# Triangle attention and window scan on one core: scores, biases and row maxima in one VectorE operation, and the output projection moved to the mixed values' bank

## The chip, the cores and the metric

The kernel runs on one core of a Trainium2 chip. The metric is the device time of one execution in microseconds (us). A core has five engines, each with its own queue of instructions that it works off in order: TensorE (PE; its weight loads are listed apart as PEld), VectorE (DVE), ScalarE (ACT), GpSimd (POOL) and SyncE (SP), which here issues most of the DMA transfers. An instruction that needs another engine's result waits for a semaphore, and all that stands behind it in its queue waits too.

## The reference

The input `x` is an image of 256 x 256 positions with 128 channels. Two layers are applied, each as `x = x + layer(group_norm(x))`. Layer 0 is a triangle attention: each of the 256 rows of the image attends within itself, with 4 heads of 32 channels, and one bias per head and pair of positions is shared by all rows.

```python
# layer 0, xn: (1, 256, 256, 128) after a layer norm
tri_bias  = jnp.einsum('bijd,dh->bhij', xn, w_tri)[:, None]
mask_bias = INF * (mask[:, :, None, None, :] - 1.0)
q = (xn @ w_q).reshape(B, I, J, H, C) * (1.0 / np.sqrt(C))
k = (xn @ w_k).reshape(B, I, J, H, C)
v = (xn @ w_v).reshape(B, I, J, H, C)
scores = jnp.einsum('bimhc,binhc->bihmn', q, k) + tri_bias + mask_bias
attn = jax.nn.softmax(scores, axis=-1)
o = jnp.einsum('bihmn,binhc->bimhc', attn, v)
g = jax.nn.sigmoid((xn @ w_g + b_g).reshape(B, I, J, H, C))
o = (g * o).reshape(B, I, J, H * C)
return o @ w_o + b_o
```

Layer 1 cuts the image into windows of 8 x 8, runs a convolution and a selective scan with 16 states over each window in four orders, and gates and projects the result. All data is float32. The change concerns layer 0 alone.

## The kernel before, in words

The kernel has these stages, one after the other: statistics of the input (`bn_stats` over all of `x`), the layer norm of layer 0 with the triangle bias (the normalised image goes to DRAM as `xn_d`), the attention, and layer 1 with its scan. On the page the attention lies between about 540 and 2,735 us, layer 1 from about 2,800 us to the end.

In the attention a `Row` is one row of the image (256 positions) and a `Pair` is two rows (512 positions), since the projections to queries, keys, values and gates work on 512 columns at once. What a pair does: `load` brings `xn` and the mask, `queries`, `keys`, `values` and `gates` are matmuls on TensorE, and the functions of the same names with `_out` take their results out of PSUM. What a row does:

- `bias` (GpSimd, L449) adds the triangle bias and the mask bias of the row into `tm`, 8 blocks of 128 x 256: 4 heads, and two halves of the row's queries.
- `scores` (TensorE, L462) computes queries times keys into two PSUM tiles `sc0` and `sc1`, two heads each (4 blocks of 256 columns).
- `add(hp)` (VectorE, L472) adds `tm` to the scores of one tile, 128 x 1024 elements, into `at` in SBUF.
- `peak(hp)` (VectorE, L480) takes the negated maximum of each of the 4 blocks into `nmax`.
- `exps` (ScalarE, L488) computes the exponential of each block with `nmax` as bias, and the block's sum through ScalarE's accumulator.
- `turn(hp)` (TensorE, L516) transposes the blocks, two heads at a time, into the tiles `aT_p0` and `aT_p1`; `turn_out` copies one of them with VectorE (L528) and the other with ScalarE (L530).
- `mix` (TensorE, L539) multiplies by the values into the pair's `o_p`.
- `invert` (VectorE, L498) and `widen` (GpSimd, L503) make the reciprocal sums and spread them over the head's channels; `shares` (TensorE, L409) turns them for a pair, and `shares_out` (VectorE, L416) multiplies them into the gate.
- For a pair, `gather` (VectorE, L420) multiplies the mixed values by the gate, `project` (TensorE, L424) is the output projection into `y_p`, `project_out` (VectorE, L427) adds bias and residual, and `store` takes statistics and writes the rows to DRAM. `logistic` (ScalarE, L131 to L133) is the sigmoid of the gate.

The order of all this is written out by hand, under `tc.manual_schedule()`: the instructions stand in the queues as the loop over `s` (one step for each row) issues them. In step `s` the row `s` (`now`) is added and exponentiated, row `s + 1` (`nxt`) gets its scores, row `s - 2` (`mid`) is turned, row `s - 3` (`old`) is mixed. The pairs' work is split over the even and the odd step: `ahead` is the next pair, `behind` the last one, `done` the one before that. Two steps are one pair.

All eight PSUM banks are taken: `sc0` and `sc1` two each, `aT_p0` and `aT_p1` one each, one for `o_p` (pool `ps_o`), and one side bank that the results of all projections pass through in turn:

```python
        def side0(name):
            return ps_m.tile([P, 512], F32, name=name, tag="m")
```

Each tenant of the side bank is written by TensorE and emptied by one copy or operation before the next one may be written. Before the change its tenants in a pair are `g_p`, `q_p` and `y_p` in the even step, and `k_p`, `rd_p` and `v_p` in the odd one.

Of the kernel before, what the change touches and what calls it, by code (L numbers as in the profile page):

```python
# [12 lines left out]
F32 = mybir.dt.float32  # L13
AF = mybir.ActivationFunctionType
ALU = mybir.AluOpType
AX = mybir.AxisListType
# [3 lines left out]
P = 128  # L20
# [4 lines left out]
HC = 32  # L25
# [42 lines left out]
def kernel(  # L68
# [28 lines left out]
    nc = tc.nc  # L97
# [31 lines left out]
    def logistic(e):  # L129

        nc.scalar.activation(e, e, AF.Exp, scale=-1.0)  # L131
        nc.scalar.activation(e, e, AF.Ln, bias=one)
        nc.scalar.activation(e, e, AF.Exp, scale=-1.0)  # L133
# [34 lines left out]
    for dh in range(2):  # L168
        nc.scalar.dma_start(
            out=wtap[:, dh], in_=conv_w[:, dh * P : (dh + 1) * P].rearrange("t d -> d t")  # L170
# [5 lines left out]
    for dh in range(2):  # L176
        for k in range(KD):
            o, back = k % 2, k // 2
            for at, lo, n in (
# [5 lines left out]
                    out=wx[:, dh, o, at : at + n],  # L185
# [4 lines left out]
    for back in range(2):  # L190
        at = 32 * back
        nc.scalar.dma_start(
            out=wdt[at : at + DTR], in_=dt_w[:, 2 * back : 2 * back + 2]
        )
        for o in range(2):
            for dh in range(2):
                j = 2 * (o + 2 * back) + dh
                nc.scalar.dma_start(
                    out=wdt[at + DTR : at + DTR + 1, o, dh * P : (dh + 1) * P],
# [61 lines left out]
    with tc.tile_pool(name="lnc", bufs=1) as cp, tc.tile_pool(  # L261
        name="lnx", bufs=3
    ) as xp, tc.tile_pool(name="lnt", bufs=3) as tp, tc.tile_pool(
        name="lnp", bufs=2, space=PSUM
# [9 lines left out]
        for k in range(KD):  # L274
            for nh in range(2):
                for blk in range(NBLK):
                    nc.scalar.dma_start(
                        out=bdiag[k][nh][blk].rearrange("p t n -> p (t n)"), in_=zero
# [33 lines left out]
    with tc.tile_pool(name="atc", bufs=1) as cp, tc.tile_pool(  # L312
        name="atx", bufs=7
    ) as xp, tc.tile_pool(name="att", bufs=3) as tp, tc.tile_pool(
        name="ats", bufs=8
    ) as wp, tc.tile_pool(name="atps", bufs=1, space=PSUM) as ps_s, tc.tile_pool(
        name="atpt", bufs=1, space=PSUM
    ) as ps_t, tc.tile_pool(name="atpm", bufs=1, space=PSUM) as ps_m, tc.tile_pool(
        name="atpo", bufs=1, space=PSUM
# [11 lines left out]
        for mc in range(2):  # L331
            nc.sync.dma_start(
                out=trib[:, :, mc, :],
# [3 lines left out]
        def side0(name):  # L337
            return ps_m.tile([P, 512], F32, name=name, tag="m")

        class Pair:  # L340
# [24 lines left out]

            def queries_out(self):
                self.qs = tp.tile([P, 512], F32, name="qs")
                nc.scalar.mul(self.qs, self.q_p, 1.0 / math.sqrt(HC))

            def keys(self):  # L370
                self.k_p = side0("k_p")
# [48 lines left out]
                nc.vector.tensor_mul(self.og, self.o_p, self.gate)  # L420

            def project(self):
                self.y_p = side0("y_p")
                nc.tensor.matmul(self.y_p, wo, self.og, start=True, stop=True)  # L424

            def project_out(self):
# [8 lines left out]
        class Row:  # L435
# [32 lines left out]
                        )  # L468

            def add(self, hp):  # L470
                self.at[hp] = wp.tile([P, 4, IMG], F32, name="at")
                nc.vector.tensor_add(  # L472
                    self.at[hp],
                    self.sc[hp].rearrange("p h m n -> p (h m) n"),
                    self.tm[:, 4 * hp : 4 * hp + 4],
                )

            def peak(self, hp):
                self.nmax[hp] = wp.tile([P, 4], F32, name="nmax")
                nc.vector.tensor_reduce(  # L480
                    self.nmax[hp], self.at[hp], AX.X, ALU.max, negate=True
                )

            def exps(self, hp, js):
                if hp == 0 and js[0] == 0:
                    self.den = wp.tile([P, NH, 2], F32, name="den")
                for j in js:
                    nc.scalar.activation(  # L488
                        self.at[hp][:, j, :],
                        self.at[hp][:, j, :],  # L490
                        AF.Exp,
                        bias=self.nmax[hp][:, j : j + 1],
                        accum_out=self.den[:, 2 * hp + j // 2, j % 2 : j % 2 + 1],
                    )

# [36 lines left out]
            def mix(self):  # L532
                pair = self.pair
                if self.r == 0:
                    pair.o_p = ps_o.tile([P, 512], F32, name="o_p")
                for n in range(2):
                    for h in range(NH):
                        base = h * HC
                        nc.tensor.matmul(  # L539
                            pair.o_p[base : base + HC, self.row],  # L540
                            pair.vs[:, self.r, n, base : base + HC],
                            self.aT[h][:, n, :],
                            start=(n == 0),
                            stop=(n == 1),
                        )
# [4 lines left out]
        def pick(items, i):  # L550
            return items[i] if 0 <= i < len(items) else None

        with tc.manual_schedule():
            for pair in pairs[0:4]:
                pair.load()
            first = pairs[0]
            first.mask_bias()
            rows[0].bias()
            rows[1].bias()
            first.queries()  # L560
            first.queries_out()
            first.keys()
            first.keys_out()
            rows[0].scores()
            first.values()
            first.values_out()
            for s in range(n_rows + 4):
                sg, odd = divmod(s, 2)
                now, nxt, mid, old = (
                    pick(rows, s),  # L570
                    pick(rows, s + 1),
                    pick(rows, s - 2),
                    pick(rows, s - 3),
                )
                ahead, behind, done = (
                    pick(pairs, sg + 1),
                    pick(pairs, sg - 1),
                    pick(pairs, sg - 2),
                )
                if not odd:  # L580
                    if sg + 4 < n_pairs:
                        pairs[sg + 4].load()
                    if behind:
                        behind.load_residual()
                    if ahead:
                        ahead.mask_bias()
                if s + 2 < n_rows:
                    rows[s + 2].bias()
                if old:
                    old.mix()  # L590
                if now:
                    now.add(0)
                    now.peak(0)
                if mid:
                    mid.turn(0)
                if now:
                    now.exps(0, [0])
                if done:
                    if odd:
                        done.project_out()  # L600
                    else:
                        done.gather()
                if mid:
                    mid.turn_out(0)
                if now:
                    now.exps(0, [1, 2, 3])
                if odd and ahead:
                    ahead.keys()
                    ahead.keys_out()
                if not odd and behind:  # L610
                    behind.gates()
                    behind.gates_out()
                if now:
                    now.add(1)
                if mid:
                    mid.turn(1)
                    mid.turn_out(1)
                if now:
                    now.peak(1)
                if odd and behind:  # L620
                    behind.shares()
                    behind.shares_out()
                if not odd and ahead:
                    ahead.queries()
                    ahead.queries_out()
                if now:
                    now.exps(1, [0, 1, 2, 3])
                if nxt:
                    nxt.scores()
                if odd and ahead:  # L630
                    ahead.values()
                    ahead.values_out()
                if not odd and done:
                    done.project()
                if odd and done:
                    done.store()
                if not odd and behind:
                    logistic(behind.gate)
                if 0 <= s - 1 < n_rows:
                    rows[s - 1].invert()  # L640
                    rows[s - 1].widen()
# [636 lines left out]
    with tc.manual_schedule():  # L1278
# [37 lines left out]
        for i, unit in enumerate(units):  # L1316
            j, place = divmod(i, per_job)
# [102 lines left out]
```

## Time and profile before

| | us |
|---|---|
| Time before, median of 3 runs (24,755.36 to 24,756.92) | 24,756.14 |
| Profiled execution: time | 24,756.32 |
| Profiled execution: span from first to last instruction | 24,754.5 |
| Busy over the whole span: PE / DVE / ACT / POOL | 23,738.4 / 22,137.9 / 18,874.1 / 21,878.7 |
| L488 (exponentials, ACT), 2,048 instructions | 1,019.2 |
| L480 (maxima, DVE), 512 instructions | 622.0 |
| L472 (additions, DVE), 512 instructions | 614.4 |
| L449 (biases, POOL), 256 instructions | 1,166.3 |

A line of the page's groups reads: source line, engine, operation, names of the output and the inputs, their shapes, the number of instructions; then busy us in total and mean ns of one; then the engine's idle time just before them, and what ended most of it. A line of the waits reads: who waited, for whom, us in total, times, longest. A line of the timeline reads: start in us from the span's beginning, duration in us, engine, line, operation, names, shapes, and in brackets the idle time before it and what ended it. The record of one instruction reaches a little beyond the start of the next one on the same engine, so a sum of records is larger than the time that they take; starts to next starts are the better price. PEclk is the granted TensorE clock as a share of full speed.

### The profile page before, as it was taken

What the parts mean: (1) busy time and instruction counts of PE and PEld (TensorE: products, weight loads), DVE (VectorE), ACT (ScalarE), POOL (GpSimd) and SP (SyncE); (2) the same over time, 40 slices, a digit from 0 to 9 for tenths busy, and PEclk for the clock granted to TensorE, in tenths of its full rate; (3) what the DMA queues carried; (4) which work ended last, traced back from release to release, by engine and by line L of the source; (5) the groups of instructions that cost most, each with busy time, mean ns of one, the idle gap of its engine ahead of it and who ended that gap; (6) DMA issues with size and microseconds to landing.
All of it is one profiled execution on the core that took longest, in us unless ns stands there. A gap on an engine that the chain in (4) does not pass through costs nothing.

```text
span 24754.5 us, 429436 instructions
## 1 busy us (share of the span) xinstructions
PE 23738.4 (96%) x171020; PEld 17003.5 (69%) x171020; DVE 22137.9 (89%) x14740; ACT 18874.1 (76%) x35334; POOL 21878.7 (88%) x10062
## 2 busy tenths in 40 slices
PE   7888899999999999999999999999999999999999
PEld 2555577777777777777777777777777777777776
DVE  6888899999999999999999999999999999999998
ACT  5777777777777777777777777777777777777776
POOL 3666699999999999999999999999999999999999
PEclk9999999999999999999999999999999999999999
DMA  5222344444444444444444444444444444444444
GB/s 192 63 63 62 101 155 156 156 153 155 155 155 154 152 155 156 156 155 152 155 155 155 155 154 154 156 156 154 153 154 156 155 154 155 153 155 156 155 154 143
DMA packets 2000343, 3638.88 MB, mean 147 GB/s; under 512 B 1129584, under 2 KB 1131760, under 8 KB 1725824
## 3 DMA queue, kind: packets, MB, share of 16 engines
q1 hardware_dynamic: 1985616, 3602.35, 43.1%
q8 instruction: 1346, 22.05, 0.4%
q10 hardware_dynamic: 12720, 9.07, 0.1%
q14 instruction: 661, 5.41, 0.1%
HBM read 3467.33 MB, written 143.65 MB: 146 GB/s over the span
## 4 chain that ended last, share of the span: by engine, by line
PE 82%; DVE 8%; ACT 6%; issue 2%; POOL 1%; DMA 0%; ACTq 0%; SPq 0%; DVEq 0%; POOLq 0%
PE b_p L1173 31%; PE y_p L1206 28%; DVE h L1189 5%; PE cv_p L762 5%; PE dt_p L1011 4%; ACT at L488 2%; PE xd_p L942 2%; PE dut_p L1045 2%; PE in_p L717 1%; PE o_p L878 1%; PE y_p L1064 1%; PE z_p L796 1%; PE u_p L915 1%; PE sc L462 1%; POOL h L1195 1%
## 5 line engine op out<-in xcount | busy, mean ns | idle before, releaser
L1195 POOL TENSOR_TENSOR h<-h,cc 128x1024 f32<-128x1024 f32 x8192 | 19182.8, 2369 | 1524.1 <-DVE h L1189 1514.1
L1189 DVE TENSOR_TENSOR_SCAN h<-da,b_p 128x1024 f32<-128x1024 f32 x8192 | 18346.7, 2274 | 2068.7 <-PE b_p L1173 2011.5
L1160 ACT ACTIVATE da<-dt,am 128x508 f32<-128x508 f32 x16384 | 10663.9, 708 | 1910.4 <-DVE h L1189 1899.3
L1173 PE MATMUL b_p<-diag,dut 64*128 64x256 f32 x65536 | 9139.4, 401 | 388.2 <-DVE h L1189 386.8
L1206 PE MATMUL y_p<-ident,h 128*128 128x128 f32 x65536 | 8168.1, 278 | 7.7 <-POOL h L1195 7.6
L1206 PEld LDWEIGHTS y_p<-ident,h 128*128 128x128 f32 x65536 | 7207.2, 142 | 1406.7 <-issue 1062.0
L1173 PEld LDWEIGHTS b_p<-diag,dut 64*128 64x128 f32 x65536 | 5700.1, 186 | 3303.5 <-issue 1848.3
L734 ACT ACTIVATE tap<-xin,wtap 128x512 f32<-128x512 f32 x2048 | 1519.6, 742 | 0.5
L762 PE MATMUL cv_p<-ident,tap 128*128 128x128 f32 x9216 | 1446.1, 280 | 31.1 <-ACT tap L734 27.1
L1021 ACT ACTIVATE sp<-dt_p 128x512 f32<-128x512 f32 x1024 | 610.3, 596 | 1079.2 <-PE dt_p L1011 1078.4
L1034 POOL TENSOR_TENSOR du<-dt,u 128x512 f32<-128x512 f32 x1024 | 1308.6, 1278 | 59.9 <-DMA z<-bt 57.0
L762 PEld LDWEIGHTS cv_p<-ident,tap 128*128 128x128 f32 x9216 | 1037.9, 141 | 390.4 <-issue 204.9
L1151 ACT ACTIVATE da<-ident 128x16 f32<-128x16 f32 x1536 | 349.3, 227 | 1202.2 <-DVE h L1189 1202.1
L488 ACT ACTIVATE at<-at,nmax 128x256 f32<-128x256 f32 x2048 | 1019.2, 501 | 240.0 <-DVE nmax L480 240.0
L449 POOL TENSOR_TENSOR tm<-trib,mb 128x2048 f32<-128x2048 f32 x256 | 1166.3, 4556 | 10.7
L1011 PE MATMUL dt_p<-xd,wdt 9*128 9x512 f32 x2048 | 1149.6, 641 | 2.5 <-DVE dt L1027 2.2
L503 POOL COPY wide<-rden 128x256 f32<-128x256 f32 x256 | 101.6, 397 | 828.5 <-DVE rden L498 826.6
L1054 ACT COPY dut<-dut_p 128x512 f32<-128x512 f32 x1024 | 589.0, 575 | 256.9 <-PE dut_p L1045 245.2
L1022 ACT ACTIVATE sp<-sp,one 128x512 f32<-128x512 f32 x1024 | 739.6, 722 | 33.7
L1027 DVE SCALAR_TENSOR_TENSOR dt<-sp,dt_p 128x512 f32<-128x512 f32 x1024 | 677.9, 662 | 15.4 <-DMA z<-bt 11.5
L516 PEld LDWEIGHTS aT_p<-ident,at 128*128 128x128 f32 x4096 | 450.8, 141 | 343.0 <-issue 142.6
L472 DVE TENSOR_TENSOR at<-sc,tm 128x1024 f32<-128x1024 f32 x512 | 614.4, 1200 | 57.7 <-POOL wide L503 30.3
(132 smaller groups left out, 16405.1 us busy)
## 6 DMA issues: line engine op xcount, KB each, us to landing
cc<-c_d SPq DMA_DIRECT2D x2048, 1024.0 KB
diag<-z SPq DMA_DIRECT2D x1024, 1024.0 KB
xt<-in_x_dram SPq DMA_DIRECT2D x16, 2048.0 KB
xt<-in_x_dram SPq DMA_DIRECT2D x32, 1024.0 KB
xn_d<-xn SPq DMA_DIRECT2D x32, 1024.0 KB
xn<-xn_d SPq DMA_DIRECT2D x128, 256.0 KB
mb<-in_mask_dram SPq DMA_DIRECT2D x128, 256.0 KB
xr<-in_x_dram SPq DMA_DIRECT2D x128, 256.0 KB
```

The lines of the kernel that those rows point to most:

```text
L449: nc.gpsimd.tensor_add(self.tm, trib.rearrange("p h m n -> p (h m) n"), self.pair.mb[:, self.row].unsqueeze(1).to_broadcast([P, 2 * NH, IMG]),
L488: nc.scalar.activation(self.at[hp][:, j, :], self.at[hp][:, j, :], AF.Exp, bias=self.nmax[hp][:, j : j + 1], accum_out=self.den[:, 2 * hp ...
L734: nc.scalar.activation(scaled.rearrange("p s (y x) -> p s y x", x=WIN), self.xin[:, dh] .rearrange("p y f x -> p (y f) x")[:, 2 * dy : 2 * ...
L762: nc.tensor.matmul(cv_p[:, s], now[:, s], ident, start=(tap == 0 and s == 0), stop=(tap == 8 and s == GS - 1), is_transpose=True, skip_gro ...
L1011: nc.tensor.matmul(token_order(self.dt_p), wdt[rows, self.o, dh * P : (dh + 1) * P], token_blocks(self.xd[rows]), start=True, stop=True,)
L1022: nc.scalar.activation(sp, sp, AF.Ln, bias=one)
L1034: nc.gpsimd.tensor_mul(token_blocks(du), token_order(self.dt[back][dh]), token_blocks(self.u[:, dh]),)
L1160: nc.scalar.activation(da[:, :, j, lo:hi], dt[:, :, lo:hi], AF.Exp, scale=am[:, a0 : a0 + 1])
L1173: nc.tensor.matmul(b_p[:, s, :, h * 64 : (h + 1) * 64].rearrange("p n t -> p t n"), job.dut[self.back][rows, p, h, self.dh * P : (self.dh ...
L1189: nc.vector.tensor_tensor_scan(out=out_, data0=d0, data1=d1, initial=0.0, op0=ALU.mult, op1=ALU.add)
L1195: nc.gpsimd.tensor_mul(self.h, self.h, cc.rearrange("p n s t -> p s n t"))
L1206: nc.tensor.matmul(job.y_p[:, 2 * p + s, self.dh * P : (self.dh + 1) * P], self.h[:, s, j], ident, start=(first and s == 0 and j == 0), st ...
```

## The change

`add` no longer issues one addition over four blocks followed by `peak`'s maximum. It issues four `tensor_tensor_reduce`, one for each block of 128 x 256: the block is the sum of scores and biases, times -1, and the smallest of these negated sums, which is the negated maximum, goes to `nmax`. `exps` gets `scale=-1.0` so that the exponential is taken of the same number. `peak` is gone. The scaled copy of the queries `qs` goes from ScalarE to VectorE.

The order is changed as well: `y_p` is written to the bank of `o_p` (both have the tag "o", one buffer), `project` and `project_out` follow `queries_out` in the even step, `keys` goes from the odd step to the end of the even one, and `shares` goes ahead of `turn(1)` in the odd step, while `shares_out` stays behind `turn_out(1)`. The side bank's tenants are now `g_p`, `q_p`, `k_p` in the even step and `rd_p`, `v_p` in the odd one. Nothing else differs; layer 1 and the stages ahead of the attention are untouched.

```diff
--- before.py
+++ after.py
@@ -365,7 +365,9 @@
 
             def queries_out(self):
                 self.qs = tp.tile([P, 512], F32, name="qs")
-                nc.scalar.mul(self.qs, self.q_p, 1.0 / math.sqrt(HC))
+                nc.vector.tensor_scalar(
+                    self.qs, self.q_p, 1.0 / math.sqrt(HC), None, ALU.mult
+                )
 
             def keys(self):
                 self.k_p = side0("k_p")
@@ -420,7 +422,8 @@
                 nc.vector.tensor_mul(self.og, self.o_p, self.gate)
 
             def project(self):
-                self.y_p = side0("y_p")
+
+                self.y_p = ps_o.tile([P, 512], F32, name="y_p", tag="o")
                 nc.tensor.matmul(self.y_p, wo, self.og, start=True, stop=True)
 
             def project_out(self):
@@ -468,18 +471,20 @@
                         )
 
             def add(self, hp):
+
                 self.at[hp] = wp.tile([P, 4, IMG], F32, name="at")
-                nc.vector.tensor_add(
-                    self.at[hp],
-                    self.sc[hp].rearrange("p h m n -> p (h m) n"),
-                    self.tm[:, 4 * hp : 4 * hp + 4],
-                )
-
-            def peak(self, hp):
                 self.nmax[hp] = wp.tile([P, 4], F32, name="nmax")
-                nc.vector.tensor_reduce(
-                    self.nmax[hp], self.at[hp], AX.X, ALU.max, negate=True
-                )
+                for j in range(4):
+                    nc.vector.tensor_tensor_reduce(
+                        out=self.at[hp][:, j],
+                        in0=self.sc[hp][:, j // 2, j % 2],
+                        in1=self.tm[:, 4 * hp + j],
+                        scale=-1.0,
+                        scalar=3.0e38,
+                        op0=ALU.add,
+                        op1=ALU.min,
+                        accum_out=self.nmax[hp][:, j : j + 1],
+                    )
 
             def exps(self, hp, js):
                 if hp == 0 and js[0] == 0:
@@ -490,6 +495,7 @@
                         self.at[hp][:, j, :],
                         AF.Exp,
                         bias=self.nmax[hp][:, j : j + 1],
+                        scale=-1.0,
                         accum_out=self.den[:, 2 * hp + j // 2, j % 2 : j % 2 + 1],
                     )
 
@@ -532,7 +538,7 @@
             def mix(self):
                 pair = self.pair
                 if self.r == 0:
-                    pair.o_p = ps_o.tile([P, 512], F32, name="o_p")
+                    pair.o_p = ps_o.tile([P, 512], F32, name="o_p", tag="o")
                 for n in range(2):
                     for h in range(NH):
                         base = h * HC
@@ -590,23 +596,18 @@
                     old.mix()
                 if now:
                     now.add(0)
-                    now.peak(0)
                 if mid:
                     mid.turn(0)
                 if now:
                     now.exps(0, [0])
-                if done:
-                    if odd:
-                        done.project_out()
-                    else:
-                        done.gather()
+                if done and not odd:
+                    done.gather()
                 if mid:
                     mid.turn_out(0)
                 if now:
                     now.exps(0, [1, 2, 3])
-                if odd and ahead:
-                    ahead.keys()
-                    ahead.keys_out()
+                if odd and behind:
+                    behind.shares()
                 if not odd and behind:
                     behind.gates()
                     behind.gates_out()
@@ -615,14 +616,14 @@
                 if mid:
                     mid.turn(1)
                     mid.turn_out(1)
-                if now:
-                    now.peak(1)
                 if odd and behind:
-                    behind.shares()
                     behind.shares_out()
                 if not odd and ahead:
                     ahead.queries()
                     ahead.queries_out()
+                if not odd and done:
+                    done.project()
+                    done.project_out()
                 if now:
                     now.exps(1, [0, 1, 2, 3])
                 if nxt:
@@ -630,8 +631,9 @@
                 if odd and ahead:
                     ahead.values()
                     ahead.values_out()
-                if not odd and done:
-                    done.project()
+                if not odd and ahead:
+                    ahead.keys()
+                    ahead.keys_out()
                 if odd and done:
                     done.store()
                 if not odd and behind:
```

## The prediction

> **What bounds the kernel now.** I began with the page's share of the span by engine and its chain of waits. The chain says where the end is set, and it is mostly not here:
>
> ```profile
> PE 82%; DVE 8%; ACT 6%; issue 2%; POOL 1%; DMA 0%; ACTq 0%; SPq 0%; DVEq 0%; POOLq 0%
> ```
>
> TensorE holds 82% because layer 1 fills the span from about 2,800 us on, and the diff does not touch layer 1. So only the attention stage can move, and its own busy times are needed (busy us of each engine in a stretch, then TensorE's granted clock):
>
> ```profile
> core 0: us, PE busy (x) PEld busy (x) DVE busy (x) ACT busy (x) POOL busy (x), PEclk, DMA share, GB/s
> 540.00:2735.00 2195.00, 1885.18 (x14844) 1132.10 (x14844) 1936.22 (x2430) 1739.26 (x5375) 1338.99 (x639) 0.96 0.21 61
> ```
>
> VectorE is the busiest (1,936 of 2,195 us), TensorE next; DMA is at 0.21. The stage is a loop over 128 pairs of rows. `gates_out` (L399) runs once in each; its first and last starts in the timeline are 561.35 and 2726.93 us, so one pair takes 2165.6 / 127 = **17.05 us**. The single intervals are of two kinds, 16.43 to 16.44 and 18.0 us. The groups of instructions between 1,000 and 2,600 us, shapes kept apart, give what the change replaces:
>
> ```profile
> L488 ACT ACTIVATE at<-at,nmax 128x256 f32<-128x256 f32 x1501 | 747.0, 501 | 176.9 <-DVE nmax L480 176.9
> L480 DVE TENSOR_REDUCE nmax<-at 128x4 f32<-128x1024 f32 x376 | 456.8, 1215 | 6.5
> L472 DVE TENSOR_TENSOR at<-sc,tm 128x1024 f32<-128x1024 f32 x375 | 449.8, 1200 | 23.1 <-POOL wide L503 22.2 <-PE sc L462 0.9
> ```
>
> Addition and maximum are two passes over the same 1,024 elements and together nearly half of VectorE's work. The waits in that stretch (total us, times, longest) show what else costs time:
>
> ```profile
> DVE gate L416 <- PE rd_p L409: 124.3, 94, 1.6
> PE rd_p L409 <- ACT ks L376: 130.8, 94, 1.4
> PE k_p L372 <- DVE xr L427: 58.0, 93, 0.6
> ACT at L488 <- DVE nmax L480: 176.9, 188, 1.1
> ```
>
> Once per pair VectorE waits 1.3 us for the turned shares `rd_p`, which wait for ScalarE to empty the one side bank of `k_p`; `k_p` itself waited for `xr`, because `y_p` lay in the same bank. ScalarE waits for maxima. The timeline of TensorE in an interval of 16.44 us, then in the next, of 18.02 us:
>
> ```profile
> 1529.38 0.63 PE L409 MATMUL rd_p<-ident,wide 128*128 128x128 f32 x4 [1.40 <-ACT ks L376]
> 1529.94 1.15 PE L462 MATMUL sc<-ks,qs 32*128 32x256 f32 x16
> 1531.01 1.16 PE L381 MATMUL v_p<-wv,xn 128*128 128x128 f32 x8
> ...
> 1545.81 0.63 PE L409 MATMUL rd_p<-ident,wide 128*128 128x128 f32 x4 [1.39 <-ACT ks L376]
> 1546.37 2.09 PE L462 MATMUL sc<-ks,qs 32*128 32x256 f32 x16
> 1548.39 1.80 PE L381 MATMUL v_p<-wv,xn 128*128 128x128 f32 x8
> ```
>
> The same matmuls take nearly twice as long: TensorE runs a moment at half speed, right after the gap that `rd_p` leaves. (2165.6 - 127 x 16.44) / 1.58 = 49 such moments, 78 us in the stage.
>
> [...]the addition's starts lie 1.14 us ahead of the next instruction's[...], and 128 copies of two elements take 9.00 us together, 70 ns each:
>
> ```profile
> 1.41 9.00 DVE L223 COPY perm<-ident 128x2 f32<-128x2 f32 x128
> ```
>
> [...]No accumulator read on VectorE is in this trace.[...]
>
> **The change, part by part**, per pair, in starts to next starts from the timeline.
>
> *Fused operation.* Out go 4 additions at 1.14 us and 4 maxima (two at 1.13, two at 1.21, which wait for their addition): 9.24 us. In come 16 operations on 128x256 and, as the two programs' orders show, behind each an accumulator read, none with a wait between the two. Price of one couple: [...]70 ns for the read as for the small copies: **0.41 us**, an estimate. Bounds: below, 0.40 (nothing shorter than 256 columns and two fixed costs is in sight). Above, if the read waits until its operation's record has ended (records reach 75 ns past the next start): 0.49; with a read as long as ScalarE's record of 191 ns: 0.61; [...]as the scan L1189 runs (1,024 elements in 2,274 ns), 0.53 + 0.08 + 0.08 + 0.07 = 0.76. I take 0.41 to 0.45: [...]on ScalarE, where L488 has the same accumulator, the read starts 0.40 us behind its operation, before its record of 0.50 has ended, and costs 0.09.
>
> *Queries' copy to VectorE.* `qs` leaves ScalarE (0.50) and comes to VectorE at 0.61, as the aT copies of equal shape. It stands behind the aT copy; what is queued behind it is `xr` and the reciprocal, and `keys` waits for it, since it frees the side bank.
>
> *Output projection in the mixed values' bank, keys to the even step, shares ahead of turn(1).* No instruction is added. The side bank has five tenants instead of six, `keys` no longer waits for `xr` (0.62 per pair), and the shares are turned when the keys' copy is a good half step back, so the 1.40 of `rd_p` and VectorE's 1.3 behind it go. New waits: the next pair's `o_p` needs `xr` done. In my order of starts `xr` ends about 0.3 us before `mix` could begin, behind sc and k_p; if VectorE is slower, TensorE waits there. Shares need POOL's `wide`: POOL has 2 x (4.56 + 0.40) + 0.62 = 10.5 us of work per pair, below every period considered, and is free when the reciprocal comes. SyncE's loads keep their places; the residual is used one step sooner, still two steps (over 14 us) behind its issue. The sign turned in the exponential is an immediate: nothing.
>
> *Sums per pair.* VectorE before: 9.24 + aT 4 x 0.60 + gate 0.66 + xr 0.66 + og 0.61 + shares 0.61 + bn 0.60 + reciprocals 0.22 = 15.0, plus the 1.3 wait and small ones = 16.4, which is the short interval. After: 15.0 - 9.24 + 0.61 + 16 x 0.41 = **12.9**. ScalarE: 13.0 - 0.5 = 12.5. TensorE, unchanged: mix 2.0, turns 4.0, q, y, k, g 3.9, sc 2.2, v 1.1, shares 0.56 = **13.7**. TensorE is then the longest. What stays late: the second half of turn(1) waits for the copy of turn(0) on ScalarE or VectorE, about 0.3 us in each step, since one bank per head is shared by both. So 13.7 + 0.6 = **14.3 us**. With the 1.4 gap gone I count no half-speed moments.
>
> The stage gives back 127 x (17.05 - 14.3) = 349 us. Against the profiled execution (span 24,754.5, time 24,756.3, 0.2 above the median): **24,407 us**, 1.4% less.
>
> **The rivals.** (A) As above, period 13.8 to 14.6, also with the half-speed moments left (one per 42.7 us, 43 x 1.58 = 67 us): 24,345 to 24,475. For it: the rates of add and reduction. 0.64. (B) The couple is dearer, 0.48 to 0.60: VectorE is the bound again, 6.4 + 16 x 0.56 = 15.3 plus 0.2 of waits = 15.5, so 24,560; over 0.48 to 0.60 some 24,440 to 24,640. For it: nothing here shows how long a read waits for its operation. 0.22. (C) **Slower**: [...]6.4 + 16 x 0.76 = 18.5 us, 127 x 1.5 = +185, so 24,940. It decides where VectorE's sum passes 17.05, at (17.05 - 6.4) / 16 = 0.67 a couple. For it: the scan's rate; against it: the reduction's. 0.08. (D) No change: a couple at about 0.67, or the fused operations being split so that ScalarE's waits come back: 0.04. (E) The change does not do what it says: the orders show the fused operations and the moves, so 0.02, time as B.
>
> **How the numbers follow.** Likeliest A: 24,407. The range runs from a period of 13.8 (24,343) to B's with 15.7 (24,585); outside lie C, D and B's end. A measurement of this kernel can tell about 0.2% (50 us) from no change. Faster: A, B but for a little, E: 0.87; same 0.05; slower 0.08.
>
> **What would show it.** Right: fused rows of about 0.42 us and reads of some 0.12 to 0.2 us in their records, starts 0.41 to 0.45 apart per couple; L399's successor once per 14.3 us; no wait of the shares for `ks`; the stage's clock at 1.00; `qs` gone from ScalarE. Wrong: fused rows near 0.65 us (C), VectorE with no idle time and sc waiting for it (B), or TensorE's granted clock below 0.96.

## The result, and the profile after

The changed kernel takes 24,396.3 us (median; 24,395.0 to 24,398.8), against 24,756.5 for the kernel before: a ratio of 0.9855 with a 95% interval of 0.9838 to 0.9872, so faster by 1.5%. The forecast was 24,407. The profiled execution has a span of 24,397.0 us.

The whole difference lies in the attention stage. The starts of `gates_out` (now L401) run from 559.34 to 2365.97 us: 1806.6 / 127 = 14.23 us per pair, against 17.05, and 127 x (17.05 - 14.23) = 359 us. All intervals but the first and the last are 14.25 us; the intervals of 18 us are gone. The windows of the stage (busy us of each engine, then TensorE's granted clock):

```profile
core 0: us, PE busy (x) PEld busy (x) DVE busy (x) ACT busy (x) POOL busy (x), PEclk, DMA share, GB/s
540.00:2376.00 1836.00, 1760.32 (x14846) 1080.36 (x14844) 1543.85 (x5630) 1645.55 (x5248) 1342.83 (x640) 1.00 0.24 74
```

VectorE's busy time has fallen by 392 us and it is now third; TensorE is busy for 1,760 of 1,836 us, and its granted clock is 1.00. The groups of the changed kernel between 1,000 and 2,300 us:

```profile
L493 ACT ACTIVATE at<-at,nmax 128x256 f32<-128x256 f32 x1461 | 726.9, 502 | 0.0
L478 DVE CUSTOM_DVE_ANT_0 at<-sc,tm 128x256 f32<-128x256 f32 x1460 | 526.2, 417 | 0.0
...
L478 DVE DVE_READ_ACCUMULATOR2_ANT nmax<- 128x1 f32 x1460 | 121.7, 83 | 0.0
```

The exponentials no longer wait for maxima (177 us of ScalarE's idle time before, none now), and their scale costs nothing that shows: 502 ns each, 501 before. The fused operation and its accumulator read are two rows, of 417 and 83 ns. What one couple of operation and read costs is seen from the starts in the timeline of VectorE:

```profile
1500.10 0.41 DVE L478 CUSTOM_DVE_ANT_0 at<-sc,tm 128x256 f32<-128x256 f32 x1
...
1500.44 0.08 DVE L478 DVE_READ_ACCUMULATOR2_ANT nmax<- 128x1 f32 x1
1500.44 0.42 DVE L478 CUSTOM_DVE_ANT_0 at<-sc,tm 128x256 f32<-128x256 f32 x1
...
1500.79 0.08 DVE L478 DVE_READ_ACCUMULATOR2_ANT nmax<- 128x1 f32 x1
1500.79 0.42 DVE L478 CUSTOM_DVE_ANT_0 at<-sc,tm 128x256 f32<-128x256 f32 x1
```

A couple starts every 0.344 us (median), and the read starts in the same hundredth as the next instruction (1500.44, 1500.79): it takes almost no time of its own. The waits of the stretch that stand where those of the kernel before stood:

```profile
ACT ks L378 <- PE k_p L374: 118.8, 91, 1.3
DVE aT L534 <- PE aT_p L522: 97.4, 91, 1.1
...
PE aT_p L522 <- ACT aT L536: 51.0, 91, 0.6
```

The direction has turned: ScalarE and VectorE now wait for TensorE. TensorE's own wait is one, 0.56 us per pair, and the timeline of TensorE shows where (the second of the two heads that turn(1) turns in the odd step, behind the shares):

```profile
1506.22 0.60 PE L411 MATMUL rd_p<-ident,wide 128*128 128x128 f32 x4
1506.73 0.66 PE L522 MATMUL aT_p<-ident,at 128*128 128x128 f32 x4
1507.94 0.66 PE L522 MATMUL aT_p<-ident,at 128*128 128x128 f32 x4 [0.56 <-ACT aT L536]
1508.53 1.15 PE L465 MATMUL sc<-ks,qs 32*128 32x256 f32 x16
```

The shares `rd_p` start without a wait. The list holds no wait of `mix` for `xr`, and TensorE shows no idle time before `o_p` or `y_p`, so their shared bank costs nothing that shows.

### The profile page after: what moved, and what is told of

Its sections match the earlier page's. It is cut to its first block, busy times and chain, and to the rows that moved or that the text cites. A ratio compares the mean times of both kernels' runs of the same rounds, so it can differ in the third digit from the quotient of the medians.

```text
span 24397.0 us, 432632 instructions
## 1 busy us (share of the span) xinstructions
PE 23614.0 (97%) x171020; PEld 16953.5 (69%) x171020; DVE 21743.9 (89%) x17940; ACT 18780.0 (77%) x35206; POOL 21891.4 (90%) x10062
## 4 chain that ended last, share of the span: by engine, by line
PE 85%; DVE 7%; ACT 5%; issue 2%; POOL 1%; DMA 0%; ACTq 0%; DVEq 0%; SPq 0%; POOLq 0%
PE b_p L1175 31%; PE y_p L1208 28%; DVE h L1191 5%; PE cv_p L764 5%; PE dt_p L1013 4%; PE xd_p L944 2%; PE dut_p L1047 2%; PE in_p L719 1%; PE aT_p L522 1%; PE sc L465 1%; PE o_p L880 1%; PE y_p L1066 1%; POOL h L1197 1%; PE z_p L798 1%; PE u_p L917 1%
## 5 line engine op out<-in xcount | busy, mean ns | idle before, releaser
L1191 DVE TENSOR_TENSOR_SCAN h<-da,b_p 128x1024 f32<-128x1024 f32 x8192 | 18343.9, 2274 | 2074.1 <-PE b_p L1175 2023.1
L478 DVE CUSTOM_DVE_ANT_0 at<-sc,tm 128x256 f32<-128x256 f32 x2048 | 738.1, 417 | 8.1 <-PE sc L465 7.7
L522 PE MATMUL aT_p<-ident,at 128*128 128x128 f32 x4096 | 579.9, 279 | 70.6 <-ACT aT L536 70.6
```

The lines of the kernel that those rows point to most:

```text
L522: nc.tensor.transpose(aT_p[:, n, mc * P : (mc + 1) * P], self.at[hp][:, 2 * hh + mc, n * P : (n + 1) * P], ident,)
L1191: nc.vector.tensor_tensor_scan(out=out_, data0=d0, data1=d1, initial=0.0, op0=ALU.mult, op1=ALU.add)
```

## The experiments

My theory was: VectorE's two passes and TensorE's wait at the side bank both cost before, the wait also by halving TensorE's clock now and then; after the change TensorE's own work sets the period. The rivals: only VectorE's work mattered, or only the order did; and the half-speed moments have another cause. Periods below are the intervals between the starts of `gates_out`.

**The fused operation alone.** The kernel before, with `add` and `exps` of the changed one; besides them, only `peak` and its calls go (the new body of `add` is as in the diff of the change and left out here):

```diff
                         bias=self.nmax[hp][:, j : j + 1],
+                        scale=-1.0,
...
                     now.add(0)
-                    now.peak(0)
...
-                if now:
-                    now.peak(1)
```

> Kernel before with the fused operation alone (order, banks and the queries' copy on ScalarE as before). Theory (both halves of the change pay, and TensorE's loop with its waits sets the period): VectorE falls to about 11.3 us of work per pair, but the shares still wait for the keys' copy in the side bank, so TensorE's 13.7 us of work keep gaps of about 1.3 us (rd_p) and more: a period of 15.2 to 15.4 us instead of 17.05, and half-speed moments of TensorE still there behind the rd_p gap. Time 24,520 to 24,610 us. Rival 1 (VectorE's work was all that mattered): period near 14.3, time about 24,400 as in the changed kernel. Rival 2 (only the bank and the order mattered): within 50 us of 24,756.

24,524.6 us, ratio 0.9906 (0.9892 to 0.9921); all intervals but the first and the last are 15.24 us. The waits between 1,000 and 2,300 us:

```profile
DVE gate L416 <- PE rd_p L409: 136.2, 85, 1.6
...
PE rd_p L409 <- ACT ks L376: 117.9, 85, 1.4
```

The wait at the side bank stays, 1.39 us a pair, as expected, and the period is the expected 15.2. But the expected half-speed moments are missing, although the 1.39 us gap of TensorE is there: the stage's clock is 1.00. A gap of this size alone does not bring them here. This refutes that part of the expectation, and the experiment on the small gap below follows from it.

**The order and the banks alone.** The changed kernel with the separate addition and maximum, `peak(0)` behind `add(0)` and `peak(1)` behind `turn_out(1)`, and `qs` back on ScalarE (of the edit only the calls of `peak` are shown):

```diff
                 if now:
                     now.add(0)
+                    now.peak(0)
...
                     mid.turn_out(1)
+                if now:
+                    now.peak(1)
```

> Changed kernel with separate addition and maximum again, and the queries' copy back on ScalarE: the order and the banks alone. Theory: VectorE's 15.0 us of work per pair bound it without the wait of 1.3 us for rd_p: period 15.0 to 15.2, all intervals alike (no half-speed moments, since the gap of TensorE is split up): time 24,495 to 24,530. Rival 1 (VectorE's passes were the whole gain): within 80 us of 24,756. Rival 2 (half-speed moments come from low use of TensorE as a whole, which is 13.7 of 15.1 here, not from one gap): intervals of two kinds remain, time about 24,570.

24,495.8 us, ratio 0.9895 (0.988 to 0.991); intervals of 15.0 us, nearly all alike, and the stage's clock 1.00. The waits of the same stretch:

```profile
ACT at L489 <- DVE nmax L481: 116.2, 173, 1.0
...
PE aT_p L517 <- ACT aT L531: 93.5, 87, 1.1
```

No wait of VectorE is left in the list at all: its 15.0 us of work per pair is the period, to the tenth. So each part alone gains about as much as the other (232 and 261 us), and together 360, less than their sum, because both take away the same half-speed moments (78 us) and each lays bare the next limit. The three moves of the order (the bank of `y_p`, the keys, the shares) were tried together only; what each is worth alone is open.

**The queries' copy back on ScalarE.** The changed kernel with one line as before:

```diff
-                nc.vector.tensor_scalar(
-                    self.qs, self.q_p, 1.0 / math.sqrt(HC), None, ALU.mult
-                )
+                nc.scalar.mul(self.qs, self.q_p, 1.0 / math.sqrt(HC))
```

> Changed kernel with the queries' scaled copy back on ScalarE. Theory (TensorE sets the period; both VectorE and ScalarE have slack): period 14.25 as in the changed kernel, time within 20 us of it, 24,380 to 24,415. Rival (ScalarE's relief of 0.5 us per pair is part of the gain): period 14.7, about 24,460. Rival (the copy delays keys and xr on VectorE, so that it costs): below 24,370.

24,396.9 us, the changed kernel's time to within 1 us; period 14.25. In this order it makes no difference which of the two engines does this copy.

**TensorE twice.** The changed kernel with the keys' matmul issued twice:

```diff
-                nc.tensor.matmul(self.k_p, wk, self.xn, start=True, stop=True)
+                for _ in range(2):
+                    nc.tensor.matmul(self.k_p, wk, self.xn, start=True, stop=True)
```

> Changed kernel with the keys' matmul issued twice for each pair into the same tile: 0.86 to 0.97 us more of TensorE, same output. Theory (TensorE sets the period): period 15.1 to 15.25, time 24,396 + 127 x 0.9 = 24,510 (24,500 to 24,525). Rival (TensorE has slack, the chain of waits through VectorE or ScalarE sets the period): less than 60 us more.

24,505.2 us; period 15.11, so 0.86 us more. In the changed kernel the gates' matmul `g_p`, of the same shape, takes 0.86 us from its start to TensorE's next one (1498.37 to 1499.23), so by this price the whole of the added work shows. TensorE's work and its one wait (0.56 us in the changed kernel) set the period.

**More work for VectorE.** The changed kernel, and in each step ahead of `invert`:

```diff
+                for _ in range(2):
+                    nc.vector.bn_stats(spare, trib.rearrange("p h m n -> p (h m n)")[:, 0:512])
```

> Changed kernel with two more bn_stats on 512 elements in each step on VectorE, into a spare tile: 2.4 us more of VectorE per pair. Theory (VectorE's sum is 11.9 us after the change, 2.3 below the period): most of it is swallowed, period 14.25 to 14.5, time 24,396 to 24,430. Rival (VectorE still sets the period): 127 x 2.4 = 305 us more, about 24,700.

24,422.3 us; period 14.44. Of 2.4 us of added work per pair 0.19 show, as a new wait of TensorE for VectorE's copy of a turned head (18.1 us in 90 pairs). VectorE had more than 2 us of slack.

**The gap before the shares filled.** The kernel before with 8 useless transposes per pair where TensorE waits for the side bank (the transposes of the last head in odd steps, issued three times):

```diff
-                    for n in range(2):
+                    again = 3 if hp == 1 and hh == 1 and self.r == 1 else 1
+                    for n in list(range(2)) * again:
```

> Kernel before with useless work: the four transposes of the last head are issued three times in odd steps, 8 more per pair, 1.0 us of TensorE, in the place where TensorE waits 1.4 us for the side bank. The output is the same. Theory (the half-speed moments come from this gap): all intervals of about 16.44 us, the 49 moments gone, TensorE's clock in the stage 1.00 instead of 0.96, time about 24,756 - 78 = 24,680, faster although work was added. Rival (the moments have another cause, such as a fixed beat or the load): two kinds of intervals as before, time 24,756 or up to 130 us more if the added transposes delay the copies behind them.

24,676.5 us, ratio 0.9968 (0.9955 to 0.998): 80 us faster with 1,024 transposes more. All intervals but a few at the ends are 16.43 or 16.44 us. The windows of the stage:

```profile
540.00:2655.00 2115.00, 1914.05 (x15866) 1184.39 (x15866) 1926.11 (x2430) 1733.49 (x5374) 1338.21 (x639) 1.00 0.22 64
```

The clock is 1.00 where it was 0.96. The half-speed moments need TensorE's idle time at this place: of the 1.39 us gap 0.52 are left (50.4 us in 97 pairs).

**Only the small gap filled.** The fused operation alone had the big gap and no such moments, so something else must differ. In the kernel before, the wait of 0.34 us in turn(1) lies about 1 us ahead of the gap of 1.39; in the fused one neither that small wait nor the one of 0.62 us before `k_p` exists. Three of the third head's four transposes are issued again there, and the big gap is left:

```diff
-                    for n in range(2):
-                        for mc in range(2):
+                    blocks = [(n, mc) for n in range(2) for mc in range(2)]
+                    if hp == 1 and hh == 0 and self.r == 1:
+                        blocks = blocks + blocks[:3]
+                    for n, mc in blocks:
```

> Kernel before with three of the four transposes of the third head issued again in odd steps: 0.38 us of useless TensorE work per pair in the small gap of 0.34 us (wait for ScalarE's copy) that lies 1 us ahead of the big one; the big gap of 1.4 us before rd_p is left as it is. Theory (after e1, which had the 1.4 us gap and no half-speed moments: what counts is the idle time that falls in one stretch of 3.4 us, 1.73 us in the kernel before and 1.4 in e1): the moments go, all intervals 16.44, time about 24,680. Rival (the gap of 1.4 us is enough in this order, and e1 escaped for another reason): intervals of two kinds, time 24,740 to 24,770.

24,678.3 us, ratio 0.9968 (0.9955 to 0.998), intervals of 16.43 but for a few at the ends. TensorE's waits between 1,000 and 2,600 us, and the stage's windows:

```profile
PE rd_p L409 <- ACT ks L376: 134.8, 97, 1.4
PE k_p L372 <- DVE xr L427: 60.3, 97, 0.6
```

```profile
540.00:2655.00 2115.00, 1844.21 (x15228) 1114.18 (x15228) 1936.01 (x2430) 1733.09 (x5375) 1340.28 (x639) 1.00 0.22 63
```

The big wait is unchanged, and so is the one of 0.62 us before `k_p`; the moments are gone. Closing 0.34 us of idle time per pair (43 us in all) gives 80 us. So the gap of 1.39 us alone is not enough: the idle time of both gaps, 1.73 us, has to come together.

The trace of the kernel before also shows in which stretch, and why only some of the pairs are hit. Its records of the half clock start on a fixed grid of 3.41 us, which shifts against the loop of 16.44 us. Three stretches of this grid, the first ahead of the shares at 1529.38, the other two around those at 1545.81 (behind the stretch's length stands TensorE's busy time; its clock is the third figure from the end):

```profile
1525.86:1529.27 3.41, 1.78 (x10) 0.92 (x8) 2.98 (x4) 3.41 (x12) 1.56 (x1) 1.00 0.65 226
1542.93:1546.34 3.41, 1.68 (x13) 1.09 (x11) 2.35 (x3) 3.41 (x12) 0.93 (x1) 1.00 0.92 242
1546.34:1549.75 3.41, 3.41 (x23) 2.58 (x23) 2.58 (x4) 1.78 (x8) 1.51 (x3) 0.50 0.11 41
```

In the first the grid cuts the big gap, TensorE is idle for 1.63 us, and no slow moment follows. In the second both gaps lie whole, TensorE is idle for 1.73 us, and the third runs at half clock. The same holds through the stage, worked out from the trace's gaps and clock records: of the 629 stretches from 575 to 2,727 us, the 50 with 1.72 us or more of idle time are each followed by one at half clock, and the 579 others, with at most 1.64, are not. At the start of the stage one stretch with 0.99 us of idle time (from 570.13) is followed by one at half clock; it ran at half clock itself. With the fused operation alone the list of waits has one of TensorE, of 1.39 us (117.9 us in 85 pairs). With the small gap filled it has those of 1.39 and 0.62 us; in the trace of the kernel before 2.57 us lie between the two (1525.42 to 1527.99), so a stretch of 3.41 us that holds all of the longer one does not reach the other: 1.39 us of the two at most, an estimate from the starts of that trace.

**The copy first.** The experiments on TensorE point to its last wait. In odd steps ScalarE copies the turned head before the first exponential:

```diff
-                if now:
+                if now and not odd:
                     now.exps(0, [0])
...
-                    now.exps(0, [1, 2, 3])
+                    now.exps(0, [0, 1, 2, 3] if odd else [1, 2, 3])
```

> Changed kernel, and in odd steps ScalarE copies the turned head before the first exponential instead of after it. Theory (TensorE's 13.7 us plus its one remaining wait, 0.56 us for ScalarE's copy in odd steps, make the period of 14.25): the copy comes 0.49 us sooner, the period falls to about 13.8, time 24,396 - 127 x 0.45 = 24,340 (24,330 to 24,350). Rival (ScalarE's order doesn't matter, the limit lies elsewhere): within 15 us of 24,396.

24,375.1 us; period 14.08, a gain of 21 us where 56 were expected. The timeline of TensorE:

```profile
1508.00 1.39 PE L522 MATMUL aT_p<-ident,at 128*128 128x128 f32 x8
1509.32 1.19 PE L465 MATMUL sc<-ks,qs 32*128 32x256 f32 x16
1510.66 1.13 PE L383 MATMUL v_p<-wv,xn 128*128 128x128 f32 x8 [0.16 <-DVE gate L418]
```

The eight transposes still take 1.39 us in place of 1.09, since ScalarE is now busy with the gate's logistic until 1508.11 and only then copies; and the values now wait 0.16 us for the shares' product on VectorE, which they do not in the changed kernel.

**The logistic earlier.** On top of it, the logistic goes ahead of the second half's exponentials in the even step:

```diff
+                if not odd and behind:
+                    logistic(behind.gate)
                 if now:
                     now.exps(1, [0, 1, 2, 3])
...
-                if not odd and behind:
-                    logistic(behind.gate)
```

> The kernel with the copy first in odd steps, and the gate's logistic on ScalarE moved ahead of the second half's exponentials in even steps, where ScalarE would otherwise stand idle 1.3 us later, waiting for the keys. Theory (TensorE's sum of 13.7 us sets the period, the copy of the turned head still came late because it stood behind the logistic): TensorE's last wait in turn(1) goes, period 13.75 to 13.9, time 24,375 - 127 x 0.25 = 24,343 (24,330 to 24,358). Rival (the logistic ahead of the exponentials delays the keys' copy and the shares behind it): 24,375 or more.

24,365.7 us, ratio 0.9842 (0.9826 to 0.9858), period 14.00: the fastest of these versions, 31 us below the changed kernel. The gain over the version before it is 9 us, where 32 were expected. The timeline of TensorE:

```profile
1503.06 1.09 PE L522 MATMUL aT_p<-ident,at 128*128 128x128 f32 x8
1504.08 1.48 PE L465 MATMUL sc<-ks,qs 32*128 32x256 f32 x16
1505.72 1.13 PE L383 MATMUL v_p<-wv,xn 128*128 128x128 f32 x8 [0.16 <-DVE gate L418]
```

The transposes run through in 1.09 us, but the scores behind them take 1.48 in place of 1.15. That they wait inside for VectorE to empty the second score tile is an estimate that fits the timeline, whose last fused operation of the step ends as VectorE's aT copy starts at 1504.29; no run tested it.

## Why the prediction was right

- **The bound.** The stage's windows and the waits named two costs that depend on each other, VectorE's passes and the side bank. The fused operation alone gives 15.24 and the order alone 15.0: both were real, neither enough.
- **The period after.** TensorE's sum was put at 13.7 us and its last waits at 0.6. Measured: 14.25, of which 0.56 is a wait, so 13.69. The sum was right within a few hundredths (the terms as printed add up to 13.8). The wait was right in size by luck: it lies in the odd step alone, 0.56 us, and not with 0.3 in each step, as the prediction had it. That TensorE sets the period is shown by its doubled matmul (+0.86 us) and by the added work of VectorE (+0.19 of 2.4).
- **The couple of operation and read.** This term was too high: 0.41 to 0.45, measured 0.344, under even the lower bound of 0.40. What it leaves for the operation itself, 0.34, was an estimate of mine, as were the terms of the bounds, and the trace before gives about as much: 0.60 us from start to start for VectorE's copies of 512 columns and 1.14 for the additions of 1,024, so an estimated 0.33 for 256. That part fits; the read, priced at 70 ns like the small copies, adds almost nothing, and its record is 83 ns, not 120 to 200. So VectorE's sum after is 11.9, not 12.9. It made no difference to the time, because TensorE was the longest either way: with 2.4 us of work added to those 11.9, the period grew by only 0.19. The rivals in which the couple is dearer (B) or runs at the rate of the scan L1189 (C; 2,274 ns for 1,024 columns, twice the addition's 1.14 us) are out.
- **The queries' copy** was priced at 0.61 on VectorE (measured 0.60, start to next start) and hidden; the run without it shows that it is.
- **The half-speed moments.** The prediction blamed the gap before the shares for 49 of them, 78 us, and let them go with it (the trace has 50 intervals of 18.0 us). They went, and filling the gap alone gains 80 us. But the gap alone is not what brings them: with its 1.39 us and without the small wait ahead of it the stage's clock is 1.00 in two runs, and only with both, 1.73 us of idle time in one stretch of the trace's 3.41 us grid, does the next one run at half clock. TensorE need not be idle all through such a stretch: 1.72 us are enough here.
- **The new wait** of `o_p` for `xr`, the margin of 0.3 us, never bound: in the trace around 1,500 us `xr` ends at 1503.41 and `mix` starts at 1504.28, so the margin is about 0.9 us.
- The forecast of 24,407 was 11 us too high; the mean interval of 14.23 in place of 14.3 is 127 x 0.07 = 9 of them.

## What to carry to other kernels

Lay out a loop's work per engine by starts to next starts, add the waits that remain, and take the longest (here TensorE's 13.69 + 0.56 = 14.25 us): a change that frees one engine is worth only the distance to the next sum, and two changes that free different engines need not add up (232 and 261 us alone, 360 together). Look at TensorE's short gaps together with its clock: here two gaps of 0.34 and 1.39 us lay about 1 us apart from start to start, and closing the smaller was worth more than its length, even with useless work (80 us for 43 us of gaps). With TensorE as the bound, moving ScalarE's copy and logistic earlier bought only part of what was expected (21 of 56 us, then 9 of 32), because the next late producer stood right behind it.

## What the runs showed of the hardware

- An accumulator read on VectorE behind the operation that fills it took 83 ns in its record and almost none of the engine's time: the next instruction started with it, and couples started 0.344 us apart. On ScalarE the read had a record of 192 ns, and the next instruction started 0.09 us behind it (1500.45 and 1500.54).
- The fused addition and running minimum of 256 columns, with the scores in PSUM, took 0.344 us with its read, where the two passes took 0.28 to 0.30 each per 256 columns (1.13 to 1.21 us for 1,024), so 0.57 to 0.59 together.
- TensorE ran at half clock for 3.41 us after each stretch of the trace's 3.41 us grid in which its idle time added up to 1.72 us or more (gaps of 0.34 and 1.39 us), and not after those with at most 1.64 (50 and 579 stretches from 575 us on; ahead of them one with 0.99, itself at half clock, was followed by another). Only these gaps were tried. That the grid of the clock records is also the one in which idle time is counted was read from one trace, and no run varied it.
